# The final weighted sum of a token router moved from VectorE to GpSimd

## The chip, the cores and the metric

The kernel runs on one core of one Trainium2 chip. The metric is the time of one execution on the device, in microseconds (us). The engines of the core are TensorE (PE in the profile; PEld is its weight load), VectorE (DVE), ScalarE (ACT), GpSimd (POOL) and SyncE (SP, which here only orders transfers). Each engine works through its own list of instructions, and semaphores tie the lists together.

## The reference, cut to what matters

The program is a Fourier layer network over 64 images of 256 x 256, followed by one transformer layer over 333 tokens of 256 features for each image (256 image rows and 77 text rows). The change lies in the last part of that layer, the feed-forward with routing. Only the 165 tokens with the highest router weight pass through it:

```python
weights = (jnp.einsum('bsd,do->bso', x, wr) + br)[..., 0]
k = max(1, int(CAPACITY * s))
kk = k - 1 if k > 1 else 1
_, idx = jax.lax.top_k(weights, k)
sel_idx = idx[:, :kk]
sel = jnp.take_along_axis(x, sel_idx[:, :, None], axis=1)
h = jax.nn.gelu(jnp.einsum('bkd,dh->bkh', sel, w1) + b1)
y = jnp.einsum('bkh,hd->bkd', h, w2) + b2
y = y * w_sel[..., None]
processed = jnp.zeros_like(x).at[batch_idx, sel_idx].set(y)
return processed + x
```

Here `x` is the normalized hidden state, and the caller adds the hidden state itself once more. So each output row is: the row of `y` that belongs to the token (a row of zeros for tokens not kept) times the token's router weight, plus the residual.

## The kernel before, in words

The first three quarters of the time go to the Fourier layers, with an order of work that the source fixes by hand. They don't contain the changed lines. After them comes the loop of lines 1135 to 1152, once for each of the 64 images `b`. Everything is float32. Within the loop the order on each engine is set by a scheduler that places the instructions by their readiness and the order of the source; the instructions of several images are mixed.

The 333 tokens of an image lie in three tiles, `t` = 0, 1, 2, with 128, 128 and 77 rows (partitions) of 256 elements. The steps of an image are these.

- `image_rows` (line 889) ends the Fourier part for an image two ahead. SyncE orders eight transfers `ch` of 1 MB each (line 909) into a pool of seven buffers; TensorE reduces each one with four matmuls (line 911).
- `attention` (line 1003) normalizes, multiplies and forms scores (line 1023), takes their maximum (line 1028, VectorE) and exponential (line 1030, ScalarE), applies them (lines 1037 to 1061), adds the residual to give `h1` (line 1064), and normalizes that to `z`. GpSimd adds a bias to the hidden state (line 1057) and stores `z` to memory (line 1069).
- `select` (line 947) computes the router weight of each token and ranks the tokens by comparisons, on VectorE (lines 955 to 982). It yields `fw` (the weight, or zero), `idx` (the token's place among the kept ones) and `place` (a matrix of ones and zeros).
- `fetch` (line 985) turns `place` into a list of row numbers `who` with small matmuls (line 994) and asks, from GpSimd, for the kept rows of `z` by an indirect transfer in two pieces, of 83 and 82 rows (line 998, tile `zr`). It is called in the midst of the next image's `attention`.
- `feed_forward` (line 1072) transposes these rows (line 1079), applies the two weight matrices (lines 1087 and 1098, with the gelu on ScalarE at line 1091 between them), and transposes back to `ys` (line 1108). GpSimd stores the rows to memory (line 1111, tensor `yr`), and asks for them again by token, three indirect transfers into the tile `o` (line 1115). It also adds `z` to `h1` (line 1118).
- `finish` (line 1121) is called one image later. It forms `o * fw + h1` for each of the three tiles and stores the result in 17 transfers from GpSimd, sixteen of 16 KB (line 1129) and one of 77 KB (line 1133).

GpSimd thus issues, in one list, the stores of `z` and `ys`, both kinds of indirect fetches, and all stores of the result, beside six additions an image. The built program gives its transfers eight semaphores in turn, so a transfer may have to wait until the one issued eight before it has landed. In the list of before, six of the result's stores stand between the fetch of `o` and the fetch of `zr`, and the other eleven behind the latter.

Buffers: `o` has two, `h1` three, the small tiles `fw` and `idx` four; the memory tensors for `z` and `y` three each.

Of the kernel before, what the change touches and what calls it, by code (L numbers as in the profile page):

```python
# [12 lines left out]
ALU = mybir.AluOpType  # L13
# [125 lines left out]
def tile_fno_fusion_transformer(ctx: ExitStack, tc: tile.TileContext, a, cst_d, grid_d, out):  # L139
    nc = tc.nc  # L140
# [980 lines left out]
    def finish(b, o, h1, fw):  # L1121
        for t in range(3):
            r = rows[t]
            nc.vector.scalar_tensor_tensor(  # L1124
                o[:r, t, :], o[:r, t, :], fw[:r, t:t + 1], h1[:r, t, :], ALU.mult, ALU.add
            )
        for g in range(4):
            for n in range(4):
                nc.gpsimd.dma_start(  # L1129
                    out[b, 64 * n + 16 * g:64 * n + 16 * g + 16].rearrange("(p t) d -> p t d", t=2),  # L1130
                    o[32 * g + 8 * n:32 * g + 8 * n + 8, 0:2, :],
                )
        nc.gpsimd.dma_start(out[b, S:TOK], o[0:TXT, 2, :])
# [5 lines left out]
    for b in range(B):  # L1139
        now, got = done, []  # L1140
        if b + 2 < B:
            hs[b + 2] = image_rows(b + 2)
        if b + 1 < B:
            done = attention(b + 1, hs.pop(b + 1), lambda: got.append(fetch(b, now[-1])))
        else:
            got.append(fetch(b, now[-1]))
        if last:
            finish(b - 1, *last)
        last = feed_forward(b, *now, *got)
        if b + 1 < B:  # L1150
            done += select(b + 1, done[1])
    finish(B - 1, *last)


# [31 lines left out]
```

## Time and profile before

| What | Value |
|---|---|
| Median of 3 runs | 12645.45 us (12633.35 to 12670.76) |
| The profiled execution's own time | 12662.01 us |
| Its span, first to last instruction | 12660.2 us |
| Busy: PE, DVE, ACT, POOL | 11148.0, 8876.0, 6048.8, 2037.2 us |
| Mean granted clock of TensorE | 0.939 |
| Line 1124 (weighted sum), 192 instructions | 92.7 us, 483 ns each |
| Line 1057 (bias, GpSimd), 128 x 256 | 751 ns each |
| Line 1129 (stores of the result), 1024 instructions | 530.0 us, 518 ns each in the median |
| Line 998 (`zr`), issue to landing | 5.2 / 11.9 / 16.6 us (least, median, most) |
| Line 1115 (`o`), issue to landing | 2.7 / 8.5 / 10.2 us |

The span is the time between the first and the last recorded instruction of one execution. An engine's busy time counts its instructions but not its waits. A line of the timeline gives the start, the duration, the engine, the source line, the operation, the tile that is written and those that are read (`o<-yr,idx`), how many instructions were merged into the line (`x6`), and in brackets how long the engine had been idle before it and what ended that. The granted clock is the share of TensorE's full clock that the chip allowed. DMA is the share of the core's 16 transfer engines that was busy.

### The profile page before, as it was taken

The numbers are of one execution on the slowest core, as the hardware profiler recorded it, in microseconds if no ns is written. First come the engines' busy times: TensorE is split into PE (matmuls) and PEld (weight loads), VectorE is DVE, ScalarE is ACT, GpSimd is POOL, SyncE is SP. The second block draws the span as 40 slices with busy tenths as digits, with TensorE's granted clock in tenths as the row PEclk, the third lists the DMA queues.
The fourth block names the chain that finished last, engine by engine and source line by source line (L and its number), as shares of the span: only waits on it lengthen the run. The fifth ranks groups of instructions, "written<-read, shape, count | busy, mean of one in ns | idle before, by whom it ended". The sixth has DMA issues, their size and how long they took to land. (4 is left out here: it accounts for less than half of the span.)

```text
span 12660.2 us, 404578 instructions
## 1 busy us (share of the span) xinstructions
PE 11148.0 (88%) x181142; PEld 5823.2 (46%) x181142; DVE 8876.0 (70%) x10892; ACT 6048.8 (48%) x10153; POOL 2037.2 (16%) x2630
## 2 busy tenths in 40 slices
PE   6999999997999999999979999999996888888887
PEld 3444444443444444444434444444443555555555
DVE  6777777777777777767667767677775666666665
ACT  5555555555555555545545545555553333333333
POOL 0000000001000000000010000000001455555555
PEclk7999999998999999999989999999997899889888
DMA  6555555556899998988888989889898666666664
GB/s 226 202 201 203 201 201 200 200 201 221 350 352 353 350 354 344 352 340 349 336 314 347 351 341 355 344 338 349 348 352 286 222 223 228 226 228 232 225 224 149
DMA packets 648775, 3550.85 MB, mean 280 GB/s; under 512 B 136632, under 2 KB 187320, under 8 KB 248056
## 3 DMA queue, kind: packets, MB, share of 16 engines
q1 hardware_dynamic: 539520, 3392.85, 69.8%
q0 software_dynamic: 100368, 128.39, 4.2%
q8 instruction: 1417, 23.22, 0.7%
q10 hardware_dynamic: 7144, 3.72, 0.1%
q14 instruction: 326, 2.67, 0.1%
HBM read 1794.51 MB, written 1729.56 MB: 278 GB/s over the span
## 5 line engine op out<-in xcount | busy, mean ns | idle before, releaser
L669 ACT ACTIVATE ring<-ring 128x1024 f32<-128x1024 f32 x3072 | 3108.8, 1012 | 1192.8 <-PE ring L662 1154.5
L650 DVE STREAM_TRANSPOSE t<-vo 128x2048 f32<-128x2048 f32 x1536 | 3549.9, 2311 | 174.9 <-ACT vo L645 14.4
L662 PE MATMUL ring<-vo,w 32*32 32x512 f32 x49152 | 2852.8, 622 | 391.2 <-DVE zt L689 138.9
L645 ACT ACTIVATE vo<-ring 128x1024 f32<-128x1024 f32 x1536 | 1568.2, 1021 | 3006.2 <-PE ring L638 2392.4
L646 DVE TENSOR_SCALAR vo<-ring 128x1024 f32<-128x1024 f32 x1536 | 1858.1, 1210 | 603.6 <-PE ring L638 415.0
L679 PE MATMUL ring<-t,cst 32*32 32x512 f32 x49152 | 1874.4, 605 | 311.4 <-issue 310.6
L689 DVE STREAM_TRANSPOSE zt<-ring 128x1024 f32<-128x1024 f32 x384 | 711.5, 1924 | 1678.5 <-PE ring L679 1678.5
L597 POOL TENSOR_TENSOR ams<-am,sk 48x512 f32<-48x512 f32 x384 | 486.9, 1268 | 8650.8 <-DMA am<-mix 8331.5
L662 PEld LDWEIGHTS ring<-vo,w 32*32 32x32 f32 x49152 | 763.6, 105 | 1905.2 <-ACT ring L669 478.6
L679 PEld LDWEIGHTS ring<-t,cst 32*32 32x32 f32 x49152 | 974.6, 104 | 1172.2 <-issue 726.6
L638 PE MATMUL ring<-vin,ws 32*32 32x512 f32 x32768 | 1239.5, 608 | 23.6 <-issue 21.6
L1129 POOL DMA_DIRECT2D out_dram<-o x1024 | 530.0, 530 | 808.4 <-DVE gt L979 394.2
L702 PEld LDWEIGHTS ring<-cst,zt 128*128 128x128 f32 x4608 | 535.4, 194 | 173.3 <-ACT vo L645 162.5
L669 ACT ACTIVATION_READ_ACCUMULATOR ring<-ring 128x1 f32 x3072 | 584.2, 190 | 0.0
L702 PE MATMUL ring<-cst,zt 128*128 128x96 f32 x4608 | 567.7, 280 | 6.7 <-DVE zt L689 6.7
L911 PE MATMUL hp<-ch,win 128*32 128x512 f32 x4096 | 469.0, 602 | 12.8 <-DMA ch<-v 12.7
L638 PEld LDWEIGHTS ring<-vin,ws 32*32 32x32 f32 x32768 | 253.4, 103 | 407.9 <-issue 375.7
L608 PE MATMUL ring<-ams,cst 49*128 49x512 f32 (+1 forms) x1536 | 391.5, 621 | 34.5 <-POOL ams L597 25.0
L1023 PE MATMUL pp<-azT,qT 128*128 128x333 f32 (+1 forms) x768 | 411.5, 690 | 0.0
L1124 DVE SCALAR_TENSOR_TENSOR o<-o,fw,h 128x256 f32<-128x256 f32 (+1 forms) x192 | 92.7, 483 | 397.7 <-DMA o<-yr,idx 262.4
L994 PE MATMUL pp<-cstt,place 128*83 128x2 f32 (+3 forms) x768 | 110.3, 248 | 282.4 <-DVE place L982 264.2
L1087 PE MATMUL pp<-zs,w 128*128 128x165 f32 x2048 | 319.6, 316 | 41.2 <-DVE zs L181 24.5
(940 smaller groups left out, 12260.0 us busy)
## 6 DMA issues: line engine op xcount, KB each, us to landing
v<-vo SPq DMA_DIRECT2D x1536, 1024.0 KB
vin<-v SPq DMA_DIRECT2D x1024, 1024.0 KB
ch<-v SPq DMA_DIRECT2D x512, 1024.0 KB
mix<-ob SPq DMA_DIRECT2D x96, 512.0 KB
am<-mix SPq DMA_DIRECT2D x384, 96.0 KB
xin<-in_x_dram SPq DMA_DIRECT2D x16, 1024.0 KB
mv<-in_x_dram SPq DMA_DIRECT2D x256, 64.0 KB
zr<-fz POOLq DMA_DIRECT2D x128, 128.0 KB, 2.0
```

What stands on the lines that cost most here:

```text
L597: nc.gpsimd.tensor_tensor(ams[b % 2][hv], a_[hv], sk[hv].rearrange("p c k -> p (c k)"), ALU.mult)
L638: nc.tensor.matmul(ps[n][32 * j:32 * j + 32], lhsT=ws[32 * n:32 * n + 32], rhs=v[32 * n:32 * n + 32, 2 * j:2 * j + 2, :], start=False, sto ...
L645: nc.scalar.activation(of[:, 0:2], t2[0], AF.Relu)
L646: nc.vector.tensor_scalar(of[:, 2:4], t2[1], 0.0, None, ALU.max)
L650: nc.vector.transpose(t32[b, t // 2][:, :, 8 * (t % 2):8 * (t % 2) + 8, :].rearrange("p y s c -> p s y c"), o.rearrange("p s (y l) -> p s ...
L662: nc.tensor.matmul(ps[n][32 * j:32 * j + 32], lhsT=w4[i + 1][32 * n:32 * n + 32], rhs=o[32 * n:32 * n + 32, 2 * j:2 * j + 2, :], start=Tru ...
L669: nc.scalar.activation(t2[n], t2[n], AF.Square, accum_out=acc[:, at:at + 1])
L679: nc.tensor.matmul(ps[n][32 * j:32 * j + 32], lhsT=FYT[32 * n:32 * n + 32, k, :], rhs=t32[b, j][32 * n:32 * n + 32, k].rearrange("p s c -> ...
L689: nc.vector.transpose(zt[:, h].rearrange("p k c -> p c k"), t2[h].rearrange("p n (s c) -> p c (n s)", c=C),)
L702: nc.tensor.matmul(ps[:, 0, 96 * g:96 * g + 96], lhsT=zt[:, h, k0:k0 + 4, :].rearrange("p k c -> p (k c)"), rhs=FX[:, h, 48 * r:48 * r + 9 ...
L911: nc.tensor.matmul(hp[32 * g:32 * g + 32], lhsT=win[:, 7 - t:39 - t], rhs=ch[:, g], start=False, stop=t == 7, skip_group_check=True,)
L1129: nc.gpsimd.dma_start(out[b, 64 * n + 16 * g:64 * n + 16 * g + 16].rearrange("(p t) d -> p t d", t=2), o[32 * g + 8 * n:32 * g + 8 * n + 8 ...
```

## The change

The weighted sum of `finish` is computed by GpSimd. VectorE did it in one instruction for each tile; GpSimd takes two, a multiplication by the row's weight and an addition of the residual, both in place in `o`. The stores behind it are the same, and are still issued by GpSimd. Nothing else in the source differs.

```diff
     def finish(b, o, h1, fw):
         for t in range(3):
             r = rows[t]
-            nc.vector.scalar_tensor_tensor(
-                o[:r, t, :], o[:r, t, :], fw[:r, t:t + 1], h1[:r, t, :], ALU.mult, ALU.add
-            )
+            nc.gpsimd.tensor_scalar(o[:r, t, :], o[:r, t, :], fw[:r, t:t + 1], None, ALU.mult)
+            nc.gpsimd.tensor_add(o[:r, t, :], o[:r, t, :], h1[:r, t, :])
         for g in range(4):
             for n in range(4):
                 nc.gpsimd.dma_start(
```

In the built program the six new instructions stand on GpSimd's list behind the fetch of `o`. The first store of the result stands between the last multiplication and the last addition, six more follow, and then the fetch of `zr`, behind seven stores where there were six. On VectorE's list the three instructions in the last third of `select` are gone; in every second image the multiplication of line 893 for a later image has moved up, ahead of the last `place`. The order of TensorE's list is unchanged. All lines from 1125 on have a number lower by one.

## The prediction

> **What bounds the kernel now.** The sliced page says where GpSimd works at all: only in the last quarter of the span, where 64 images pass through attention and feed-forward. I call one turn of that loop a cycle, and count it from the transposes of line 1079 (they take the rows fetched by line 998, `zr`) to the next such transposes. Over the 55 undisturbed cycles from 10071 us on the mean is 44.66 us. The change touches nothing outside this loop, so I read one cycle, 11542.2 to 11586.0 us, in the timelines. TensorE first (start, duration, instruction, in brackets the idle time before it and who ended it):
>
> ```profile
> 11543.39 4.77 PE L1087 MATMUL pp<-zs,w 128*128 128x165 f32 x32 [0.76 <-DVE zs L181]
> 11547.99 4.67 PE L1098 MATMUL pp<-g,w 128*128 128x165 f32 x32
> ...
> 11556.08 6.22 PE L911 MATMUL hp<-ch,win 128*32 128x512 f32 x56
> ...
> 11570.02 0.31 PE L994 MATMUL pp<-cstt,place 77*83 77x2 f32 x2 [3.60 <-DVE place L982]
> ...
> 11572.73 5.70 PE L1023 MATMUL pp<-azT,qT 128*128 128x333 f32 x10
> ...
> 11586.02 0.45 PE L1079 MATMUL pp<-cst,zr 83*128 83x83 f32 x4
> ```
>
> TensorE stands still once, at line 994, for `place` of VectorE. VectorE is late because line 1124, the operation to be moved, waits in the middle of `select` for the fetched rows `o`:
>
> ```profile
> 11565.47 0.48 DVE L1124 SCALAR_TENSOR_TENSOR o<-o,fw,h 128x256 f32<-128x256 f32 x1 [3.77 <-issue]
> 11569.08 0.48 DVE L1124 SCALAR_TENSOR_TENSOR o<-o,fw,h 77x256 f32<-77x256 f32 x1 [0.52 <-DMA o<-yr,idx]
> 11569.67 0.29 DVE L982 TENSOR_SCALAR place<-cstt,gt 77x165 f32<-77x165 f32 x1
> ```
>
> So it looks as if moving line 1124 frees 3.6 us or more a cycle. But a second ring closes at the same place. GpSimd's timeline of the same cycle:
>
> ```profile
> 11560.55 0.97 POOL L1115 DMA_INDIRECT o<-yr,idx  x1 [0.30 <-issue]
> 11568.79 3.06 POOL L1129 DMA_DIRECT2D out_dram<-o  x6 [7.27 <-DVE gt L979]
> 11572.15 2.04 POOL L998 DMA_INDIRECT zr<-zr,who  x1 [0.30 <-DVE amv L926]
> 11574.50 1.43 POOL L998 DMA_INDIRECT zr<-zr,who  x1 [0.30 <-issue]
> 11575.93 3.17 POOL L1129 DMA_DIRECT2D out_dram<-o  x6
> 11585.94 2.04 POOL L1129 DMA_DIRECT2D out_dram<-o  x4 [6.84 <-DMA zr<-zr,who]
> ```
>
> `zr` is asked for by 11575.9 and is there only at 11585.9, when TensorE arrives too. The table by stretches says why (columns: stretch, its length, busy time of PE, PEld, DVE, ACT, POOL, granted clock, DMA share, GB/s):
>
> ```profile
> 11570.00:11578.00 8.00, 7.11 (x20) 4.27 (x21) 4.54 (x16) 2.84 (x6) 7.39 (x10) 0.58 1.01 421
> 11578.00:11583.00 5.00, 4.90 (x28) 3.95 (x27) 4.15 (x24) 1.06 (x3) 1.10 (x3) 0.99 1.02 361
> 11583.00:11586.00 3.00, 3.00 (x15) 2.34 (x14) 2.03 (x6) 0.00 (x0) 0.06 (x1) 1.00 0.26 89
> ```
>
> The 8 MB of `ch` that SyncE orders from 11557.9 on (as line 911 frees their buffers) fill the DMA engines until 11583, and `zr` comes out behind them. Taken cycle by cycle from the trace, the first `zr` lands 28.1 us after the first `ch` order (9 in 10 between 27.2 and 29.2), whether its issue ended 15.9 or 18.6 us after that order; the correlation is -0.3. So **the landing is set by the burst, not by when GpSimd asks**. In about half of the cycles TensorE waits for `zr` at line 1079, in the others `zr` has been there for 1 to 3 us: two rings of nearly one length.
>
> The last thing to see is the clock of 0.58 above. After the stop at line 994 TensorE runs at half clock; line 1023 pays for it. It also happens at line 1079, when `zr` is late there:
>
> ```profile
> 10250.42 0.79 PE L1079 MATMUL pp<-cst,zr 83*128 83x83 f32 x4 [2.49 <-DMA zr<-zr,who]
> 10251.73 7.40 PE L1087 MATMUL pp<-zs,w 128*128 128x165 f32 x32 [0.52 <-ACT zs L179]
> ```
>
> 7.40 us instead of 4.77 for line 1087, and there everything follows: `ys`, `yr`, line 911, the next burst.
>
> **What the Trainium skill says.** "TensorE: Matmul & The Clock Gate", Part 1: The HAM clock gate, has a free-running window of about 3.4 us; an idle one halves the clock, a busy one restores it. The trace agrees and is sharper: in this stage its clock record moves in steps of 3.41 us, all 63 drops follow a window in which TensorE was busy under 60%, and 60 of 64 returns follow a wholly busy window. The same page, Part 1, calls ACT, DVE and GPSIMD strict FIFO; the stop of VectorE at line 1124 is that. "GPSIMD Engine Reference", section 4.1 Engine selection, makes two-input elementwise work about 2 times slower on GpSimd and one-input work about line rate: here a 128x256 add takes 751 ns on GpSimd (line 1057) against 484 ns for the whole weighted sum on VectorE (line 1124), 1.6 times for half the work. "DMA: Bandwidth & Descriptors", Queues, rings and completion order, has each DMA engine take turns between its queues; that fits stores and fetches of 1.7 to 5 us in quiet that take up to 12.5 and 16.6 us in the burst.
>
> **The change part by part.** All against this profile's own 12662 us (span 12660.2); the median of the runs shown, 12645, is 17 lower, and I subtract that at the end.
>
> 1. Removed from VectorE: 3 x 0.48 = 1.45 us a cycle and the wait for `o`. In the new instruction order `select` runs through; line 974's last instance ended at 11561.7, the rest needs about 1.5 us, in every second image one more 1.1 us (line 893 is now ahead of it). `place` is then ready at 11563.3 to 11564.5, before TensorE reaches line 994 at 11566.0. TensorE saves the stop, 3.6 us, and the half clock: line 1023's 12 matmuls took 6.5 us, at the pace of line 1009 (8 in 2.9 us, same shape) 4.4, with line 994's own about 2.5 us less. TensorE would come to line 1079 some 5.5 us early, at 38.5 of the cycle.
>
> 2. Added to GpSimd: three multiplies and three adds. No multiply of this kind is in the trace; lower bound 0.25 us (line rate at 256 elements and next to no overhead), upper bound the add's 0.75; I take 0.5. The add is 0.75 to 0.84 by lines 1057 and 1118. GpSimd has been idle there for 7.3 us, and rows of `o` land at about 23, 25.5 and 26.8 of the cycle, so the first two pairs hide in the wait. After the last landing come, in the new order, a multiply 0.5, one store 0.5, an add 0.8, six stores 3.1, and only then `zr`: its first issue starts 4.9 us after the landing, against 3.1 now. GpSimd's DMAs use eight semaphores in turn, and with one store more ahead the second `zr` also waits for the first store; a store issued there lands 5.1 us later (median), about when the first `zr` issue ends, so nothing is added. Together `zr` is asked for about 2 us later, 19.4 (first) and 21 us after the `ch` order. Behind it in the queue are nine stores and line 1057, due only after `zr` has landed anyway.
>
> 3. The delay of 2 us mostly sinks into the burst (end at about 27): lower bound 0, upper bound 2; I take 0.3.
>
> 4. What TensorE saves at line 994 it now loses at line 1079: it arrives at 38.5, `zr` at 43.4 or later. A stop of 5 us always holds a window that is mostly idle, so **the half clock moves from line 1023, where it was covered, to lines 1087 and 1098, which carry the ring**. It lasts from the restart to the end of the first wholly busy window: 3.4 to 6.8 us, mean 5.1. The six cycles that had it there already started their `ch` 1.3 to 1.8 us late for one window (a late second `zr` taken off) and 2.9 for two, 0.45 us per us: 2.3 us.
>
> New cycle: 15.3 (line 1079 to first `ch`, mean of 14.9 and 15.7 in alternate images) + 2.3 + 28.1 (to `zr`) + 0.1 (to line 1079) + 0.3 = 46.1 us, against 44.66: +1.44. Over 59 cycles with a burst +85 us; the last four images have none, there GpSimd's 2 us count, +8. Sum +93: 12755 on this profile, **12740 us** on the median's scale.
>
> The contention of GpSimd's adds with VectorE (line 959 takes 1047 ns at 128x128 beside lines 1057 and 1118, 258 at 77x77) I cost at nothing: VectorE has 2 to 3 us to spare between lines 1028. Without that cover it is about 1 us a cycle.
>
> **Rivals.**
> - *Faster: the freed TensorE keeps its clock.* If it stands at line 1079 for less than about 1.5 us (other waits hold it up on the way, so that the idle time is spread), no window falls below 60%: 15.3 + 28.1 + 0.4 = 43.8, -0.86 x 59 + 8 = -43: 12600. For it: half of the cycles end on TensorE, and those are released. Against it: all the 5 us would have to vanish.
> - *No change.* The saving is used up before line 1079 (lines 1028 to 1052 bound by VectorE and ScalarE), or only one window is slow and the delay is wholly absorbed: between +10 and +30, 12655 to 12675.
> - *Much slower: the burst doesn't absorb.* GpSimd's 2 us reach the landing in full: +1.7 x 59 = 100 on top, 12840 to 12850. It decides if `zr` is issued later than the burst can still carry; 18.6 us after the `ch` order is the latest I can vouch for, and 19.4 lies just beyond.
>
> **Numbers.** Likeliest case 0.55 (its own range 12690 to 12790), much slower 0.15, no change 0.15, faster 0.15. A measurement of this kernel tells 0.3%, 38 us, from no change: faster 0.15, same 0.17, slower 0.68. The range 12620 to 12850 leaves out most of the faster case and the far end of the slow one.
>
> **What would show it.** Right: no wait of line 994 for `place`; line 1079 waits 4 to 6 us for `zr` in nearly every cycle; line 1087 takes 7 us instead of 4.8, and line 1023 some 4.4; first `ch` at about 17.6 of the cycle; landing still 28 us after it. Wrong: line 1087 at 4.8 us throughout (then faster), landing at 30 us after the `ch` order (then much slower), or TensorE still waiting at line 994.

## The result, and the profile after

The changed kernel takes 12833.44 us (median of 4 runs, 12807.40 to 12842.37) against 12647.75 us for the kernel before on the same chip (median of 4, 12633.35 to 12670.76). The ratio is 1.0142, with a 95% interval of 1.0121 to 1.0163: it is slower by 1.4%. The profiled execution took 12833.35 us (span 12831.5, mean granted clock 0.935), 171 us more than the profiled execution before.

The stop at line 994 is gone, and a longer one stands at line 1079. TensorE's timeline of one cycle after the change (start, duration, instruction, in brackets the idle time before it and who ended it):

```profile
11500.12 0.78 PE L1079 MATMUL pp<-cst,zr 83*128 83x83 f32 x4 [7.53 <-DMA zr<-zr,who]
11501.42 7.74 PE L1087 MATMUL pp<-zs,w 128*128 128x165 f32 x32 [0.52 <-ACT zs L179]
11509.00 4.67 PE L1098 MATMUL pp<-g,w 128*128 128x165 f32 x32
...
11526.71 0.54 PE L994 MATMUL pp<-cstt,place 128*83 128x2 f32 x6
...
11547.44 0.95 PE L1079 MATMUL pp<-cst,zr 83*128 83x83 f32 x4 [8.14 <-DMA zr<-zr,who]
```

Line 994 has no bracket any more. Line 1079 waits 7.53 and 8.14 us for `zr`, and line 1087 behind it takes 7.74 us; in the cycle shown of before it took 4.77. GpSimd's timeline of the same cycle:

```profile
11526.99 0.93 POOL L1124 TENSOR_SCALAR o<-o,fw 128x256 f32<-128x256 f32 x1 [3.88 <-DMA o<-yr,idx]
11528.01 0.73 POOL L1125 TENSOR_TENSOR o<-o,h 128x256 f32<-128x256 f32 x1
...
11531.08 0.92 POOL L1124 TENSOR_SCALAR o<-o,fw 77x256 f32<-77x256 f32 x1
...
11536.56 2.06 POOL L998 DMA_INDIRECT zr<-zr,who  x1 [0.30 <-issue]
11538.93 1.44 POOL L998 DMA_INDIRECT zr<-zr,who  x1 [0.31 <-DVE h L1064]
```

`zr` is asked for by 11540.4 and TensorE starts on it at 11547.4. The table by stretches of the same kernel (stretch, its length, busy time of PE, PEld, DVE, ACT, POOL, granted clock, DMA share, GB/s) shows what lies between:

```profile
11538.00:11543.00 5.00, 1.31 (x7) 0.59 (x4) 1.57 (x4) 0.00 (x0) 4.69 (x7) 0.87 1.03 394
11543.00:11546.00 3.00, 0.00 (x0) 0.00 (x0) 0.00 (x0) 0.00 (x0) 0.53 (x2) 0.50 0.92 156
11546.00:11550.00 4.00, 1.96 (x8) 1.59 (x9) 1.17 (x4) 0.30 (x1) 2.40 (x5) 0.50 0.17 38
```

TensorE does nothing for 3 us while the DMA engines are still full, and starts its feed-forward at a clock of 0.50. The three groups of matmuls that tell it for the whole loop (count, busy time and mean ns, idle time just before them and who ended it), before the change:

```profile
L994 PE MATMUL pp<-cstt,place 128*83 128x2 f32 (+3 forms) x768 | 110.3, 248 | 282.4 <-DVE place L982 264.2 <-DVE who L997 17.4
L1079 PE MATMUL pp<-cst,zr 83*128 83x83 f32 (+1 forms) x256 | 32.4, 245 | 30.0 <-DMA zr<-zr,who 29.8
L1087 PE MATMUL pp<-zs,w 128*128 128x165 f32 x2048 | 319.6, 316 | 41.2 <-DVE zs L181 24.5 <-ACT zs L179 16.8
```

and after it:

```profile
L994 PE MATMUL pp<-cstt,place 128*83 128x2 f32 (+3 forms) x768 | 70.2, 206 | 6.8 <-DVE place L982 6.1 <-DVE who L997 0.6
L1079 PE MATMUL pp<-cst,zr 83*128 83x83 f32 (+1 forms) x256 | 53.0, 352 | 504.9 <-DMA zr<-zr,who 504.5
L1087 PE MATMUL pp<-zs,w 128*128 128x165 f32 x2048 | 449.8, 399 | 36.5 <-DVE zs L181 19.8 <-ACT zs L179 16.8
```

The idle time has moved from line 994 to line 1079 and grown, and line 1087 is busy for 130 us more.

In means over the same 55 cycles the cycle grew from 44.66 to 47.25 us. It splits at the first `ch` order: that order comes 17.88 us after line 1079, against 15.51 before (+2.37), and the next line 1079 starts 29.37 us after it, against 29.15 (+0.22). So **nine tenths of the cycle's growth lie between line 1079 and the first `ch` order**, where the half clock is. 59 cycles times 2.59 us are 153 us; the last three cycles, which have no burst of `ch`, are 12.0 us longer together; the remaining 6 us are for the most part ahead of the loop's first line 1079 and behind its last (4 us).

### The profile page after: what moved, and what is told of

The parts are those of the page before. It is cut to its first block, busy times and chain, and to the rows that moved or that the text cites. A ratio compares the mean times of both kernels' runs of the same rounds, so it can differ in the third digit from the quotient of the medians.

```text
span 12831.5 us, 404585 instructions
## 1 busy us (share of the span) xinstructions
PE 11087.0 (86%) x181142; PEld 5852.9 (46%) x181142; DVE 8840.3 (69%) x10700; ACT 6077.4 (47%) x10153; POOL 2357.8 (18%) x3014
## 5 line engine op out<-in xcount | busy, mean ns | idle before, releaser
L638 PE MATMUL ring<-vin,ws 32*32 32x512 f32 x32768 | 1242.3, 608 | 21.6 <-issue 19.4
L1079 PE MATMUL pp<-cst,zr 83*128 83x83 f32 (+1 forms) x256 | 53.0, 352 | 504.9 <-DMA zr<-zr,who 504.5
L1087 PE MATMUL pp<-zs,w 128*128 128x165 f32 x2048 | 449.8, 399 | 36.5 <-DVE zs L181 19.8
L1087 PEld LDWEIGHTS pp<-zs,w 128*128 128x128 f32 x2048 | 433.8, 268 | 52.5 <-DVE zs L181 28.0
L959 DVE TENSOR_SCALAR dg<-cst,wcol 128x128 f32<-128x128 f32 (+1 forms) x192 | 161.9, 843 | 254.5 <-PE pp L960 250.8
```

Of the source, the lines that this page charges most:

```text
L638: nc.tensor.matmul(ps[n][32 * j:32 * j + 32], lhsT=ws[32 * n:32 * n + 32], rhs=v[32 * n:32 * n + 32, 2 * j:2 * j + 2, :], start=False, sto ...
L1087: nc.tensor.matmul(ps[:, :KEPT], lhsT=w1[:, dh, 128 * hb:128 * hb + 128], rhs=zs[:, dh, :], start=dh == 0, stop=dh == 1,)
```

## The experiments

Two theories stood against each other. A: the freed TensorE stops at line 1079 instead of line 994, and the half clock then falls on lines 1087 and 1098, which carry the ring (the chain of waits that leads from line 1079 over the `ch` orders and the landing of `zr` to the next line 1079). B: GpSimd's longer way from `o` to `zr` makes `zr` late. Both predict a slower kernel. All ratios are to the kernel before, run beside the experiment.

**TensorE kept busy in its stop** (the changed kernel and 16 more matmuls):

```diff
         ps = psum()
+        for n in range(16):
+            nc.tensor.matmul(ps[:, 0:TOK], lhsT=ONES, rhs=tabt("tri")[:, 0:TOK], start=True, stop=True)
+        ps = psum()
         for c, k in enumerate(kept):
```

> The changed kernel with 16 more matmuls (128x333, result unused) queued on TensorE just ahead of line 1079's transposes, so that it works while zr is on its way (about 5 us at full clock, into a stop of 7 to 8 us). Theory A (most of the loss is the half clock that the stop at line 1079 puts on lines 1087 and 1098): line 1087 goes back from about 7.5 to 4.8 us a cycle, the first ch order from 17.9 to about 15.3 us of the cycle, the cycle from 47.25 to about 44.7 us, the time to about 12680 us (12660 to 12700), that is 0.988 of the changed kernel and within 0.3% of the one before. Theory B (the loss is GpSimd's own longer work between o and zr): the matmuls sit in a wait that is there anyway, the time stays at about 12830 us. If both hold with the shares that the trace gives, about 50 us more than the kernel before are left.

Measured: 12735.54 us, ratio 1.0067 (1.0045 to 1.0089), 98 us less than the changed kernel, though it does more work. TensorE's timeline (line 1077 is the added work, 1082 and 1090 are the lines 1079 and 1087):

```profile
11514.14 9.12 PE L1077 MATMUL pp<-cstt,cst 128*128 128x333 f32 x32
11523.10 0.45 PE L1082 MATMUL pp<-cst,zr 83*128 83x83 f32 x4
11524.08 4.76 PE L1090 MATMUL pp<-zs,w 128*128 128x165 f32 x32 [0.52 <-ACT zs L179]
```

Line 1087 is back at 4.76 us, and the first `ch` order at 15.24 us of the cycle, as A says. The cycle is 45.68 us and not 44.7, because the added matmuls took 9.1 us where I had reckoned with 5 (the trace counts each of the 16 twice, `x32`): TensorE now came later than `zr` (line 1079's start 30.43 us after the `ch` order). So the same with 13 of them:

> As the run with 16 extra matmuls, with 13: those 16 took 9.1 us a cycle and made TensorE 1.1 us later at line 1079 than zr; 13 take about 7.4 us, and zr is 8 us behind TensorE. If the half clock is the whole of the loss and the landing stays at 29.3 us after the first ch order: first ch at 15.3, cycle 44.6 to 44.8 us, 12645 to 12675 us, as the kernel before. If it leaves something of the loss that GpSimd causes: 12690 us or more.

Measured: 12714.47 us, 1.0046 (1.0029 to 1.0063). By my threshold that speaks for a rest of B. The profile splits the difference of the spans (12721.2 to 12660.2, 61 us) as follows. The cycle is 45.19 us, +0.53 on the kernel before, and in it 0.26 are the first `ch` order, with some half clock left (0.9 us a cycle), and 0.27 the start of line 1079: 31 us over 59 cycles. The last three cycles take 109.3 us in place of 91.4: 18 us, of which the changed kernel has 12 without the added matmuls. The loop's first line 1079 came 12 us later in this profile. So a rest of B in the cycles with a burst is at most 0.27 us; in the last three cycles it is not excluded. Of the 2.59 us of such a cycle, 2.06 came back.

**The two halves of the change alone.** First VectorE's release, with nothing added to GpSimd (the kernel before without line 1124):

```diff
     def finish(b, o, h1, fw):
-        for t in range(3):
-            r = rows[t]
-            nc.vector.scalar_tensor_tensor(
-                o[:r, t, :], o[:r, t, :], fw[:r, t:t + 1], h1[:r, t, :], ALU.mult, ALU.add
-            )
```

> The kernel before without line 1124, the weighted sum: the fetched rows are stored as they are, so the weight and the residual are left out of the result. This is the release of VectorE alone, with nothing added to GpSimd. Theory A (the freed TensorE only moves its stop to line 1079 and gets the half clock there, on lines 1087 and 1098): no stop at line 994, a stop of 6 us or more at line 1079, line 1087 at about 7 us, first ch order at about 17.8 us of the cycle, cycle about 46.5 to 47.2 us, 12770 to 12830 us. If the release of VectorE were worth what the stop at line 994 costs and GpSimd's work were what spoiled it: 12450 to 12600 us.

Measured: 12814.74 us, 1.0126 (1.0109 to 1.0143). Its groups:

```profile
L994 PE MATMUL pp<-cstt,place 128*83 128x2 f32 (+3 forms) x768 | 70.3, 207 | 6.7 <-DVE place L982 6.1 <-DVE who L997 0.6
L1079 PE MATMUL pp<-cst,zr 83*128 83x83 f32 (+1 forms) x256 | 53.0, 352 | 526.1 <-DMA zr<-zr,who 525.8
```

The busy times are those of the changed kernel, and the idle time at line 1079 is even 21 us longer, with no weighted sum on any engine. Then GpSimd's load, with VectorE not released (two multiplications by one for each tile, behind the kernel's own sum):

```diff
                 o[:r, t, :], o[:r, t, :], fw[:r, t:t + 1], h1[:r, t, :], ALU.mult, ALU.add
             )
+            nc.gpsimd.tensor_scalar(o[:r, t, :], o[:r, t, :], ONES[:r, 0:1], None, ALU.mult)
+            nc.gpsimd.tensor_scalar(o[:r, t, :], o[:r, t, :], ONES[:r, 0:1], None, ALU.mult)
```

> The kernel before with two more multiplications by one on GpSimd for each of the three tiles of o, after VectorE's weighted sum (the result is the same): GpSimd's load alone, VectorE not released. zr is asked for about 1.5 us later. If the landing of zr is set by the burst and TensorE comes at 29.2 us after the first ch order anyway: 12650 to 12690 us. If the later asking passes on to the landing: 1.5 us x 59, about 12730 to 12750 us.

Measured: 12661.27 us, 1.0005 (0.9998 to 1.0012). Its groups:

```profile
L1079 PE MATMUL pp<-cst,zr 83*128 83x83 f32 (+1 forms) x256 | 32.0, 245 | 28.9 <-DMA zr<-zr,who 28.7
...
L994 PE MATMUL pp<-cstt,place 128*83 128x2 f32 (+3 forms) x768 | 109.3, 247 | 281.1 <-DVE place L982 259.8 <-DVE who L997 21.0
```

In this run the first `zr` issue ended 20.6 us after the first `ch` order, as late as in the changed kernel (20.0; 17.0 before), and the cycle took no harm: 44.59 us against 44.66. **The release of VectorE costs 1.3%, the work given to GpSimd nothing that shows in the time.** Only the last three cycles were longer in this profile, 102.8 us against 91.4; with the release alone they took 100.5. So B has fallen for the cycles with a burst, and either half of the change by itself brings most of the 12 us at the end.

**GpSimd's work doubled and cut**, in the changed kernel:

```diff
             nc.gpsimd.tensor_scalar(o[:r, t, :], o[:r, t, :], fw[:r, t:t + 1], None, ALU.mult)
+            nc.gpsimd.tensor_scalar(o[:r, t, :], o[:r, t, :], ONES[:r, 0:1], None, ALU.mult)
             nc.gpsimd.tensor_add(o[:r, t, :], o[:r, t, :], h1[:r, t, :])
```

> The changed kernel with one more multiplication by one on GpSimd ahead of each of the three multiplications (the result is the same): GpSimd asks for zr about 1 us later after the last o for the last tile, up to 2.6 us in all, and no other engine has more to do. Theory B with full pass-on: the landing of zr moves by 1 to 2.5 us, 12890 to 12980 us. Pass-on as in the change itself (1.15 of 2.75 us): about 12890 us (12865 to 12910). Theory A alone, with a landing that the ch burst pins: no change, 12833 us within 15.

```diff
-            nc.gpsimd.tensor_scalar(o[:r, t, :], o[:r, t, :], fw[:r, t:t + 1], None, ALU.mult)
             nc.gpsimd.tensor_add(o[:r, t, :], o[:r, t, :], h1[:r, t, :])
```

> The changed kernel without the multiplication by the weight: it stores o + h1, so the weight is left out of the result; GpSimd has three operations a cycle in place of six, VectorE none. zr is asked for about 1 us earlier than in the changed kernel after the last o, up to 2.5 us with the stores that move behind it. Theory B: the lateness of the landing, 1.15 us a cycle, goes for the most part: 12765 to 12790 us. Theory A alone: TensorE still stands at line 1079 and the half clock stays, 12800 to 12833 us. Both together: line 1087 still at about 7 us, landing between 28.2 and 29 us after the first ch order, about 12775 us; not back to 12650 in any case.

Measured: 12834.19 us (1.0147, 1.0128 to 1.0166) with nine operations a cycle, 12818.41 us (1.0133, 1.0114 to 1.0152) with three. The first `zr` issue ended 21.8 and 19.0 us after the `ch` order, and line 1079 started 29.32 and 29.28 us after it, against 29.37 with six. Between 19 and 22 us the time of asking doesn't matter.

**`zr` asked for much earlier.** In the changed kernel, sum and stores are queued behind both fetches of `zr` on GpSimd:

```diff
-            nc.gpsimd.indirect_dma_start(
+            asked = nc.gpsimd.indirect_dma_start(
                 zr[:n, c, :], None, z_d[b % 3][:, :], bass.IndirectOffsetOnAxis(ap=who[:n, c:c + 1], axis=0)
...
-            finish(b - 1, *last)
+            with tc.issue_after(asked.ins):
+                finish(b - 1, *last)
```

> The changed kernel with the weighted sum and all the stores queued on GpSimd behind the second fetch of zr, so that zr doesn't wait for o: it is asked for at about 12 to 13.5 us after the first ch order in place of 20 to 22. If the landing is pinned to the end of the ch burst whatever the time of asking: it lands still at about 28 us, the stop at line 1079 and the half clock stay, about 12735 us (12700 to 12770). If the place in GpSimd's queue decides (zr is late because it stands behind o and the stores): it lands at 24 us or earlier, line 1079 has little or no wait, line 1087 is back at 4.8 us, the cycle is 39 to 42 us, 12380 to 12500 us.

Measured: 12746.96 us, 1.0074 (1.0052 to 1.0097). The two issues ended 11.8 and 13.5 us after the `ch` order, 8 us earlier than in the changed kernel. The first piece landed at 25.2 us and the second at 28.9 (means of the paired landings), so TensorE stood twice at line 1079, for 2.7 and 3.1 us, and line 1087 still took 6.9 us. In one cycle:

```profile
11494.62 0.51 PE L1079 MATMUL pp<-cst,zr 83*128 83x83 f32 x2 [3.46 <-DMA zr<-zr,who]
11497.60 0.54 PE L1079 MATMUL pp<-cst,zr 82*128 82x82 f32 x2 [2.46 <-DMA zr<-zr,who]
11498.73 7.63 PE L1087 MATMUL pp<-zs,w 128*128 128x165 f32 x32 [0.59 <-DVE zs L181]
```

The second piece is there at 28.9 us, hardly before TensorE's start on `zr` in the changed kernel (29.4), though its request moved by 8 us. Whether the burst is what holds it, the next experiment tests.

**The burst taken out of the way.** A 4-byte transfer out of an older `zr` makes SyncE, which works its list in order, hold back the last four `ch` of an image until that `zr` has landed:

```diff
         for t in range(8):
+            if t == 4 and b - 3 in zrs:
+                nc.sync.dma_start(scrap, zrs.pop(b - 3)[0:1, 1, 0:1])
             ch = inp.tile([128, 4, 2, S], F32, name="ch")
...
-        zr = tp.tile([128, 2, D], F32, name="zr")
+        zr = zrs[b] = tp.tile([128, 2, D], F32, name="zr")
```

In the changed kernel:

> The changed kernel in which SyncE orders ch 0 to 3 of an image as before and ch 4 to 7 only after a 4-byte transfer out of the zr fetched in the cycle three images earlier, so behind the landing of zr: five transfers of 1 MB in the burst in place of eight, the other three after zr. If zr lands late because the burst stands before it: it lands 3 to 5 us after it is asked for, 23 to 25 us after the first ch order in place of 29.4, line 1079 waits 2 us or less, line 1087 is mostly at 4.8 us, cycle 39 to 42 us, 12320 to 12500 us. If zr's own path (who, GpSimd's queue, a fixed latency) sets it: landing still at 29 us, about 12830 us.

In the kernel before:

> The kernel before with the same split of the ch transfers. VectorE's line 1124 still stands between TensorE and place, so the stop at line 994 stays as far as o lands late; o lands earlier with the shorter burst. Cycle 40 to 43 us, 12380 to 12560 us. If the moved sum is worth something once the burst is out of zr's way, the changed kernel with the split is faster than this one by 1 to 2 us a cycle (60 to 120 us); if GpSimd's longer way from o to zr is then what counts, slower by up to 2.5 us a cycle.

Measured: 12586.99 us (0.9946, 0.9930 to 0.9963) for the changed kernel, 12655.95 us (1.0002, 0.9993 to 1.0011) for the one before. In the first, TensorE starts on `zr` 3.7 us after the end of its last issue, against 7.2 in the changed kernel, so the burst was what held it; but that issue ends only 39.8 us into the cycle, behind `o`, sum and stores, and the stop at line 1079 shrinks to 3.7 us and doesn't vanish. I had expected more. TensorE's timeline (line 1083 is 1079, 1091 is 1087):

```profile
11520.22 0.70 PE L1083 MATMUL pp<-cst,zr 83*128 83x83 f32 x4 [3.60 <-DMA zr<-zr,who]
11521.45 7.55 PE L1091 MATMUL pp<-zs,w 128*128 128x165 f32 x32 [0.52 <-ACT zs L179]
```

A stop of 3.6 us was enough for the half clock here. In the kernel before the split gave nothing, where I had expected 12560 us or less: line 1079 hardly waits there (7.6 us in all), the stop at line 994 is as it was (277.0 us), and the cycle is 44.6 us. So there are two rings of nearly one length, and taking one of them away alone gives nothing or less.

**Both obstacles away**, with the sum on GpSimd (the split and the order of the fourth experiment together):

> The changed kernel with both: ch 4 to 7 ordered behind zr, and on GpSimd the weighted sum and the stores queued behind both fetches of zr. zr is then asked for at about 30 us of the cycle in place of 35.5 and lands about 3.5 us later, before TensorE comes at 37 to 39 us. If the stop at line 1079 and its half clock are what holds the split kernel at 43.5 us: no stop, line 1087 at 4.8 us, cycle 37 to 39 us, 12200 to 12350 us. If TensorE gets a stop elsewhere (line 994, or line 911 for a ch that now comes late) that costs as much: cycle 42 to 44 us, 12530 to 12620 us.

and with the sum left on VectorE, queued behind the last rounding of `who` (the split as above, and the order below, which takes the wait for `o` out of VectorE's way to `place` without moving the sum):

```diff
-            nc.vector.tensor_copy(who[:n, c:c + 1], ps[:n, 2 * c:2 * c + 1])
+            named = nc.vector.tensor_copy(who[:n, c:c + 1], ps[:n, 2 * c:2 * c + 1])
...
-            finish(b - 1, *last)
+            with tc.issue_after(named.ins), tc.issue_after(asked.ins):
+                finish(b - 1, *last)
```

> The same with the weighted sum left on VectorE (the one instruction of the kernel before), queued behind the rounding of the row numbers who, and the stores behind both fetches of zr. VectorE no longer waits for o ahead of place. If the place in the order and not the engine is what counted: within 0.5% of the run with the sum on GpSimd, 12200 to 12380 us. If VectorE's wait for o now holds up lines 1028 to 1064 of attention instead: cycle 40 us or more, 12400 us and above.

and this last order alone, without the split:

> The kernel before with the order alone: the weighted sum stays on VectorE but is queued behind the rounding of who, the stores behind both fetches of zr; all ch ordered as before. Without the split the burst still lies before zr: no stop at line 994, zr asked for at about 27 us of the cycle, its two pieces landing at about 25 and 29 us after the first ch order as in the changed kernel with zr first, stop and half clock at line 1079, cycle 45.5 to 46.5 us, 12700 to 12760 us. If the order alone is what the split runs gained by: 12330 to 12450 us.

Measured: 12515.21 us (0.9881, 0.9862 to 0.9900), 12327.32 us (0.9736, 0.9719 to 0.9752) and 12754.00 us (1.0082, 1.0061 to 1.0103). With both, the stops at lines 994 and 1079 are gone on either engine, line 1087 runs in 4.8 us, and the cycle is 42.5 us with the sum on GpSimd, 39.4 with it on VectorE. The two kernels differ by 1.5%, where I had expected 0.5% at most if the place in the order and not the engine counted: the engine counts. What still stops TensorE with the sum on GpSimd shows the timeline of that kernel (line 964 is 960, 963 is 959, 1061 is 1057, 1122 is 1118):

```profile
11515.54 4.42 DVE L963 TENSOR_SCALAR dg<-cst,wcol 77x77 f32<-77x77 f32 x1
11515.78 2.08 POOL L1061 TENSOR_TENSOR h<-h,boB 128x256 f32<-128x256 f32 x3
11517.83 2.07 POOL L1122 TENSOR_TENSOR h<-h,fz 128x256 f32<-128x256 f32 x3
...
11520.01 0.71 PE L964 MATMUL pp<-dg,cst 77*128 77x77 f32 x2 [4.46 <-DVE dg L963]
```

VectorE's small operation takes 4.42 us and ends as GpSimd's six additions end; TensorE waits for it. Of its 64 instances of this size, 47 meet additions or multiplications of GpSimd in this kernel and take 2.2 us in the mean; with the sum on VectorE it is 36, at 1.2 us. I take it that GpSimd, busy longer with the sum and the stores, comes to these additions later, when VectorE needs to be quick. The same operation where GpSimd is not in its way, in VectorE's timeline of the kernel with the sum on VectorE:

```profile
11499.92 0.25 DVE L963 TENSOR_SCALAR dg<-cst,wcol 77x77 f32<-77x77 f32 x1
```

Over the whole loop TensorE stands 155.2 us for line 963 with the sum on GpSimd and 64.9 us with it on VectorE: 90 of the 188 us between the two. The rest I take to be what follows such a stop at half clock (line 906, which follows, took 2.07 us in the cycle above, and 1.13 at full clock); no run separates it.

All eight combinations (us, ratio to the kernel before):

| Sum on | as it was | `ch` split | `zr` first | both |
|---|---|---|---|---|
| VectorE | 12648 | 12656 (1.0002) | 12754 (1.0082) | **12327 (0.9736)** |
| GpSimd | 12833 (1.0142) | 12587 (0.9946) | 12747 (1.0074) | 12515 (0.9881) |

The split and the order are worth nothing or less singly on VectorE, and 2.6% together. Moving the sum alone only changes where TensorE stops; with both stops gone, GpSimd is the wrong place for it. The best version, 12327.32 us, beats both kernels.

## Why the prediction was right, and where its sizes were off

The sign and the mechanism held, and so did the wide range, 12620 to 12850 us. The narrower range of the likeliest case, 12690 to 12790, did not: the size was half of what came (+93 on its own profile's scale, +171 measured). A cycle grew by 2.59 us where 1.44 were predicted; of the 1.15 missing, 0.87 are the landing (step 3) and 0.28 the half clock (step 4). By its steps:

1. *VectorE's release ends the stop at line 994*: right. `place` is ready 23.9 us into the cycle, line 994 starts at 26.4. But I read the stop from one cycle (3.60 us) where the mean is 4.25, and the half clock behind it was under-sized: from the first line 994 to the end of line 1023 it took 12.8 us before and 4.7 after, 8.1 us less and not 6.1. So TensorE comes to line 1079 earlier and, with the later landing of step 3, stands there for 8.1 us, not 4 to 6.
2. *GpSimd's multiplication at 0.5 us, between 0.25 and 0.75*: mis-sized, and outside my bounds: 0.94 us at 128x256. The upper bound assumed, with the Trainium skill's "GPSIMD Engine Reference", section 4.1 Engine selection, that one-input work is the cheaper kind; the trace differs and decides: the one-input multiplication is slower than the two-input addition (0.73 us). `zr` was asked for at 20.0 and 22.2 us, not at 19.4 and 21. Nor was the later asking GpSimd's work alone: with VectorE's release and no sum at all, the first issue ended at 19.3. It had no consequence in the cycles with a burst, as the load put on GpSimd alone shows.
3. *The burst absorbs GpSimd's delay, 0.3 us left*: right as to GpSimd, wrong as to the sum. I took 28.1 us, the mean landing of before, plus 0.4 for the next line 1079, so 28.5; measured 29.37. This is the larger mis-sized term, 0.9 us a cycle or 51 us. It is not GpSimd's work: with VectorE's release alone it is 29.39. In the kernel before, the 18 of the 55 cycles in which TensorE's matmul really waited had a first landing of 28.7; but a wait picks out the late landings, so these cycles don't show what to expect of all. What moved the landing stays open. And that the landing doesn't depend on when GpSimd asks holds for requests that ended between 19 and 22 us; asked for by 11.8, the first piece landed at 25.2.
4. *The half clock moves to lines 1087 and 1098 and costs 2.3 us a cycle*: right in kind, but line 1098 was not touched (4.67 us in the mean, before and after): the cost lies on lines 1079 and 1087, which are busy for 0.3 and 2.0 us a cycle more. The first `ch` order came at 17.88 us against 17.6 predicted; from the prediction's base of 15.3, a mean without half clock, that is 2.6 us, and the half clock lasted 6.2 us of this part, not 5.1. What the Trainium skill says of the clock's windows in "TensorE: Matmul & The Clock Gate", Part 1: The HAM clock gate, on which this step rested, agrees with the runs here: stops of 8.1, 3.7 and twice 3 us in the mean brought the half clock, and filling the stop took it away.
5. *The last images*: 8 us predicted for GpSimd's delay; the last three cycles took 12.0 us more, and the release alone brings 9 there, the load alone 11.

Of the rivals, "the burst doesn't absorb" forecast 12840 to 12850 us, nearer to the measured time than my own number, and is wrong all the same: delay added on GpSimd, with the sum doubled or put on it alone, did not move the landing. A time that fits is no proof of its mechanism. "TensorE keeps its clock" was to be faster than before, 12600 us; with the clock kept by added matmuls the kernel is still slower, since TensorE's start on `zr` came 0.9 us later than I had it there, too (29.42 us with 13 of them), and the first `ch` order 0.5 us later. Of the signs, line 1087 (7.08 us in the mean), line 1023 (4.32), the first `ch` order and line 994 came as written; the wait at line 1079 was longer, and TensorE's start on `zr`, at 29.4, lay nearer to the 30 us that I had named as a sign of being wrong than to the 28 of being right.

## What to carry to other kernels

When an engine is freed from one wait, find the next thing that it needs before counting the gain: if that is pinned by something else, the idle time only moves, and what counts is what runs right behind its new place. Of the two rings of nearly equal length here, shortening one gave nothing; such a change is to be judged with the other one shortened as well. And before a fetch is asked for earlier, look at what fills the DMA engines in front of it: holding back part of a prefetch that nobody needed yet, together with the earlier request, gave 2.6% with the sum on VectorE, and neither gave anything alone.

## What was not expected of the hardware

- On GpSimd a multiplication of 128x256 by a value for each partition takes 940 ns and one of 77x256 takes 928, against 727 and 748 ns for the addition of two tiles of these sizes.
- In the kernel with both obstacles away and the sum on GpSimd, VectorE's line 963 takes 0.29 us in the mean where it meets no addition or multiplication of GpSimd and up to 4.6 us where it does; in the cycle shown it ends with GpSimd's whole run of six additions, not with one of them. The Trainium skill, "SBUF — State Buffer", Who interferes with whom, says that VectorE, when it uses its second pair of ports, as an operation of this kind can, contends for that pair with GpSimd, and that one of them holds it for the whole instruction; the trace agrees that VectorE is shut out, but for six instructions of GpSimd on end. That this operation uses both pairs, no run here shows.
- An indirect fetch in two pieces, asked for 1.7 us apart in the midst of the burst, landed 3.7 us apart (25.2 and 28.9 us after the first `ch` order): being asked for earlier helped the first piece only.
